# A post-norm decoder on one core: where the output bias is added to the residuals, and where two output pieces stand in the last attention unit

## Chip, cores, metric

One core of a Trainium2 chip. The metric is device time in microseconds of one execution, median of several runs; lower is better. TensorE (PE, with its weight loads PEld), VectorE (DVE), ScalarE (ACT), GpSimd (POOL) and SyncE (SP, which here issues nearly all DMAs) each run their own queue in order.

## The reference, cut to what matters

Four sequences (B=4) of 1024 tokens with 512 features, all float32:

```python
x = layernorm(x + attn(x))            # 32 channels of 16; q, k, v each two linear layers
x = layernorm(x + xattn(x, ctx, z0))  # causal convolution of two taps, LSTM-like gates
x = layernorm(x + ffn(x))             # x rounded to int8 steps, ternary weight, bias

def attn(x):
    q, k, v = (lin(lin(x, w, b), v_, c) for ...)          # split into 32 heads of 16
    o = softmax(q @ k.T / sqrt(16)) @ v
    return o.rearranged @ wo_w.T + wo_b                   # the output projection
```

The change touches `x + attn(x)`: the bias `wo_b` that is added to the residual `x`, and the pieces of the output projection; `layernorm` subtracts a mean and divides by a root.

## The kernel before

**Units.** Attention runs in 32 units u of four heads (L385): eight per batch. A unit has 32 half steps h (L822). In each, TensorE makes the natural scores of the *next* unit (`nat`, L555; VectorE takes their row maxima, L584, and from them L590 and L598 make the shifts that DMAs carry into the queries, L608 and L612) and the transposed scores of this unit (`scores`, L621; ScalarE takes the exponential, L649). Every fourth half step `weigh` (L654) multiplies a finished quarter with v (PE L664); its result is copied by ScalarE (L675) or added by VectorE (L677) into `o_sb`. Also every fourth half step, at h = 3, 7, ..., 31, one piece of other matmul work is taken from a list (L834 to L839): `v` projections, parts of the next q and k projections (`product`, L451), and, when these are used up from unit 24 on, pieces of the output projection (`out_piece`, L547).

**PSUM.** Transposed scores, weighings and all pieces take turns in four buffers of one pool (`ps_st`, L522), in the order of the program: whoever asks waits until the work that reads the buffer of four requests ago is done. The natural scores have two wider buffers (`ps_nat`), which the last unit uses for half of its scores (`stw`).

**Products.** `product` forms q and k projections by a Strassen scheme with seven products. ScalarE copies each out of PSUM (L477, L479), and GpSimd adds it to the others (L482 to L493). The products 2, 3 and 4 are copied into two `rooms` that take turns (L470 to L472), so a copy waits until GpSimd's sum from the room's former user is done. Unit 24 has seven such pieces and one output piece.

**Normalising.** A unit's `o_sb` is divided by its sums in four stages during the next unit (L840): sums out by DMA, reciprocals (L697), back by DMA in broadcast (L703), and at h=20 the product on GpSimd (L711) with the writing to HBM (L721).

**Residuals.** At h=5 of unit 24, `load_w_o`, `load_attention(0)` and `load_residual(0)` (L842 to L845) issue the transfers of the output weight, the attention output and x of batch 0; at h=5 of unit 28, the same for batch 2 (L858). `load_residual` (L93) issues the DMA of 2 MB and, for batches 0 and 2, records right behind it eight GpSimd additions of `b_o`, one for each tile of 128 tokens (L98 to L100). For batches 1 and 3 VectorE adds it later (L246). `project` (L233) runs the matmuls of an output piece and has VectorE add the result to the residual `y` (L247) and, at a tile's last piece, take statistics (L249). The first two tiles of batch 0 have two pieces of 256 columns, all others three of 176, 176 and 160 columns.

**Last unit.** Unit 31 has no next unit and runs 16 steps i with twice the scores each (L800). Its list `firsts` is the first norm of batch 0: the root on ScalarE at i=2 (`deviations`, L110, L117), which needs another function table than the exponential, and from i=3 on the normalising on VectorE (L118, L140, L121) and its sums and differences for the convolution (L185 to L191). At even i it weighs a quarter and does one output piece:

```python
if i % 2 == 0 and weighing:
    weigh(*weighing.pop(0))
...
if i % 2 == 0 and len(out_pieces) > 1:
    out_pieces.pop(0)()
if i > 1 and firsts:
    firsts.pop(0)()
```

GpSimd sums the convolution's weights (L170) in the first part of this unit. After it comes the tail: convolution, gates, second norm, feed-forward, third norm.

The order of the work within each engine's queue is that of these calls; nothing reorders it (`manual_schedule`, L326).

Of the kernel before, what the change touches and what calls it, by code (L numbers as in the profile page):

```python
# [19 lines left out]
NT = S // P  # L20
# [41 lines left out]
class Handed:  # L62
# [30 lines left out]
    def load_residual(self, b):  # L93
        nc = self.nc
        self.y[b] = self.tokens(b, f"y{b}")
        nc.sync.dma_start(self.y[b], self.a["x"][b].rearrange("(t p) f -> p t f", p=P))
        self.stats[b] = self.shared.tile([P, NT, 6], F32, tag=f"stats1_{b // 2}", name=f"stats1_{b}")
        if b % 2 == 0:  # L98
            for t in range(NT):
                nc.gpsimd.tensor_add(self.y[b][:, t, :], self.y[b][:, t, :], self.b_o)  # L100

    def means(self, stats, pool, name, t0=0, n=NT):
        mv = pool.tile(
# [148 lines left out]
def attention(ctx, tc, a, attn_d, ident, shared, hand):  # L252
    nc = tc.nc
# [23 lines left out]
    for i in range(2):  # L277
        t = (once if i else shared).tile([P, NT, NH * VW + 15], F32, tag=f"v_sb{i}", name=f"v_sb{i}")
# [9 lines left out]
    for n, pool in ((3, shared), (1, once)):  # L288
        t = pool.tile([P, 8 if n == 3 else 2, S], F32, tag=f"qk{n}", name=f"qk{n}")
# [13 lines left out]
    for n in range(2):  # L303
        t = shared.tile([P, 4, D + 1], F32, tag="u", bufs=2, name=f"x_sums{n}")
# [5 lines left out]
    for i in range(2):  # L310
        t = once.tile([P, 32], F32, tag=f"neg{i}", name=f"neg{i}")
# [4 lines left out]
    for i in range(2):  # L316
        t = rbcp.tile([P, S], F32, tag=f"rbc{i}", name=f"rbc{i}")
# [95 lines left out]
    def qk_pieces(p, which):  # L413

        parts = [(0, 176), (176, 176), (352, 176), (528, 176), (704, 160), (864, 160)]
        return [
            lambda pool=None, part=part: project(p, which, *part, packs[p][:, which, :], pool) for part in parts
        ]
# [78 lines left out]
    def products(p, which):  # L497


        rows = [(2 * p - 3, 2), (2 * p - 2, 2), (2 * p - 1, 2), (2 * p, 2)]  # L500
        if which == 1:
            rows = [(2 * p - 2, 22), (2 * p - 2, 26), (2 * p - 1, 4), (2 * p, 4)]
        for n, when in enumerate(rows):
            due.setdefault(when, []).append(lambda n=n: to_quadrants(2 * p + n, which, packs[which][:, n // 2, :]))
        return [
            [
                lambda part=part: product(p, which, *part)
                for part in parts
            ]
            for parts in (  # L510
                [(1, 0, 256), (1, 256, 256), (6, 0, 256), (6, 256, 256), (2, 0, 256), (2, 256, 256)],
                [(7, 0, 512), (5, 0, 512), (3, 0, 256), (3, 256, 256), (4, 0, 256), (4, 256, 256)],
            )
        ]
# [32 lines left out]
    def out_piece(b, t, c0, c1):  # L547
        pt = ps_st.tile([P, QW], F32, tag="st", name=f"po{b}_{t}_{c0}")
        hand.project(b, t, slice(c0, c1), pt[:, 0 : c1 - c0], quarters=True)
# [133 lines left out]
    def normalise(u, stage):  # L683
# [51 lines left out]
    out_pieces = [  # L735
        lambda b=b, t=t, c=c: out_piece(b, t, *c)
        for n, (b, t) in enumerate(outs)
        for c in ([(0, 256), (256, 512)] if n < 2 else [(0, 176), (176, 352), (352, 512)])
    ]
# [14 lines left out]
    for u in range(-1, NU):  # L754
        fill = []

        p, w = 2 * ((u + 5) // 4), (u + 1) % 4
        if p < NU // 2:
            if w % 2 == 0:
                parts = products(p, w // 2)  # L760
                if p == 14 and w == 0:


                    parts[0].pop()
                    parts[0].append(lambda: product(14, 0, 2, 256, 128))
                    parts[1].insert(0, lambda: product(14, 0, 2, 384, 128))
            fill += parts[w % 2]
        if u == -1:
            fill = folds[5:] + qk_pieces(1, 0) + qk_pieces(1, 1) + [
                piece for t in range(NT) for piece in v_pieces(0, t)  # L770
            ] + fill
        elif units[u][0] + 1 < B:
            vs = v_pieces(units[u][0] + 1, units[u][1])
            fill = fill + vs if w == 3 else vs + fill
        if w == 2 and p + 2 < NU // 2:
            due.setdefault((u, 24), []).append(lambda p=p: sum_w(p + 2, 0))
        if w == 0 and u >= 0 and p < NU // 2:
            due.setdefault((u, 24), []).append(lambda p=p: sum_w(p, 1))
        if w == 3 and p % 4 == 2 and p // 4 + 1 < B:
            due.setdefault((u, 28), []).append(lambda p=p: sum_x(p // 4 + 1))  # L780
        if u == -1:
            xts[1] = load_x(1)
        elif units[u][1] == 5 and units[u][0] + 2 < B:
            xts[units[u][0] + 2] = load_x(units[u][0] + 2)

        if u == -1:
            total, done, steps = len(fill), 0, HS // 3 + 1
            for n in range(steps):
                hs = range(3 * n, min(3 * n + 3, HS))
                for work in [nat(0, h // 2, h % 2, apart=h % 2 == 1) for h in hs]:  # L790
                    work()
                if n in (6, 7):
                    shift(0, 0, n == 6)
                until = total * (n + 1) // steps
                for piece in fill[done:until]:
                    piece()
                done = until
        elif u + 1 == NU:
            assert not fill
            for i in range(HS // 2):  # L800
                for work in [scores(u, i, i % 2), scores(u, i, 1 - i % 2, wide=True)]:
                    work()
                if i % 2 == 0 and weighing:
                    weigh(*weighing.pop(0))
                if i % 2 == 1:
                    weighing.append((u, i // 2))
                if i % 2 == 0 and len(out_pieces) > 1:
                    out_pieces.pop(0)()
                if i > 1 and firsts:
                    firsts.pop(0)()  # L810
                if i == 1:
                    hand.first_w = hand.load_conv(0, None)
                if i in (3, 5):
                    hand.load_ctx(i // 2 - 1)
                if i in (8, 9, 10, 11):
                    hand.sum_taps(hand.first_w, i - 8)
                if i < 2:
                    shift(u, 1, i == 0)
                if i in (2, 5, 8, 11) and stages:
                    stages.pop(0)()  # L820
        else:
            for h in range(HS):  # L822
                i, half = divmod(h, 2)
                for work in (nat(u + 1, i, half), scores(u, i, 1 - half)):
                    work()
                if h % 4 == 1 and weighing:
                    weigh(*weighing.pop(0))
                if h in (1, 3):
                    shift(u, 1, h == 1)
                if h in (17, 19):  # L830
                    shift(u + 1, 0, h == 17)
                for work in due.pop((u, h), ()):
                    work()
                if h % 4 == 3:  # L834
                    weighing.append((u, h // 4))
                    if fill:
                        fill.pop(0)()
                    elif u > 24 or u == 24 and h > 24:
                        out_pieces.pop(0)()  # L839
                if h in (5, 9, 13, 20) and stages:  # L840
                    stages.pop(0)()
                if h == 5 and u == 24:  # L842
                    hand.load_w_o()
                    hand.load_attention(0, big_slot(0, "big0"))
                    hand.load_residual(0)  # L845
                    hand.load_rest()
                if h == 5 and u == 27:
                    hand.load_w_f()
                if h == 21 and 27 <= u < 31:
                    hand.prepare_w_f(u - 27)  # L850
                if h == 21 and u == 29:
                    hand.prepare_rest()
                if h == 5 and u == 30:
                    hand.x1[0], firsts = hand.first_norm(0)
                    firsts.pop(0)()
                    hand.xf[0], parts = hand.fir_parts(0, hand.x1[0], shared)
                    firsts.extend(parts)
                if h == 5 and u == 28:  # L858
                    hand.load_attention(2, big_slot(1, "big2"))
                    hand.load_residual(2)  # L860
            assert not fill
        if u == -1:
            setup.close()
            atp = ctx.enter_context(tc.tile_pool(name="at", bufs=14))
            obuf = ctx.enter_context(tc.tile_pool(name="obuf", bufs=2))
            onp = ctx.enter_context(tc.tile_pool(name="onp", bufs=1))
# [332 lines left out]
```

## Time and profile before

| | |
|---|---|
| median of 3 runs | 2428.03 us (2427.8 to 2428.67) |
| the profiled execution | 2427.53 us, its span 2425.7 us, granted clock 0.999 |
| GpSimd: wait for the residual of batch 2 (L100 on DMA y) | 54.4 us, once |
| DMA of batch 0's residual: issued, first add | 1503.3 us, 1520.81 us |
| units 20, 24, 25, 28 (first exponential to first exponential) | 57.4, 63.4, 55.7, 57.3 us |
| ScalarE at L649, idle time before it for scores | 529.8 us in 497 waits |
| HBM traffic | 80.77 MB read, 18.35 MB written |

Rows of a time-ordered view have the start and the time taken, in us from the span's start, then engine, line of the kernel, operation, what is written and read, shapes, count, and in brackets the idle time of the engine just before and what ended it. Rows of the waits have us in total, times, and the longest. `part` is the PSUM tile of a product, `st` and `stw` are transposed scores, `nat` natural scores, `av` a weighing, `at` an exponential, `po` an output piece, `y` a residual, `extra` and `qk` the packed projections. A row "PE st L638 <- ACT extra L479" reads: TensorE's scores of L638 waited for ScalarE's copy of L479.

### The profile page before, as it was taken

To read this page: it belongs to the slowest core of one execution; us is meant where nothing else is said; L and a number is where in the kernel's file an instruction comes from. 1 tells how busy PE (TensorE), PEld (TensorE's weight loads), DVE (VectorE), ACT (ScalarE), POOL (GpSimd) and SP (SyncE) were. 2 spreads that over 40 slices of the span, in tenths; PEclk is the share of its full clock that TensorE was granted. 3 is DMA by queue.
4 is the path that set the end of the run, shared out by engine and by line. 5 is a ranking of instruction groups with operands and counts; after the bars stand their busy time and mean duration, and the time that the engine had idled before them with its cause. 6 is when DMAs were issued, how large, how long until landed. Compare 5 with 4: busy or idle time off the path is not lost.

```text
span 2425.7 us, 70210 instructions
## 1 busy us (share of the span) xinstructions
PE 2410.5 (99%) x30380; PEld 1626.6 (67%) x30380; DVE 1747.9 (72%) x2197; ACT 1329.0 (55%) x2593; POOL 588.5 (24%) x537
## 2 busy tenths in 40 slices
PE   9999999999999999999999999999999999999998
PEld 5556666666666666666666666566666799747994
DVE  3577777777777777777777777677777477878677
ACT  1056666666666666666666666566666723411333
POOL 5011311111122212111311201311210267422661
PEclk9999999999999999999999999999999999999999
DMA  6200112011001111111110012102200242160311
GB/s 222 59 3 17 28 23 56 17 30 26 17 17 30 21 54 22 25 21 20 27 25 17 17 34 93 41 17 48 89 17 12 81 149 87 70 226 18 122 35 70
DMA packets 80838, 121.45 MB, mean 50 GB/s; under 512 B 39072, under 2 KB 39328, under 8 KB 80528
## 3 DMA queue, kind: packets, MB, share of 16 engines
q1 hardware_dynamic: 79808, 115.77, 16.8%
q8 instruction: 239, 3.92, 0.7%
q10 hardware_dynamic: 720, 1.18, 0.1%
q14 instruction: 71, 0.58, 0.1%
HBM read 80.77 MB, written 18.35 MB: 41 GB/s over the span
## 4 chain that ended last, share of the span: by engine, by line
PE 97%; DVE 1%; POOL 0%; ACT 0%; DMA 0%; issue 0%; SPq 0%; DVEq 0%; POOLq 0%; ACTq 0%
PE nat L568 22%; PE av L664 20%; PE st L638 18%; PE part L59 8%; PE pc L948 6%; PE pa L948 6%; PE v L59 5%; PE pf L1032 4%; PE po L59 2%; PE po L241 2%; PE proj L59 1%; PE fold L377 1%; PE fold L59 1%; PE tr L1024 0%; PE nats L568 0%; POOL y L100 0%
## 5 line engine op out<-in xcount | busy, mean ns | idle before, releaser
L584 DVE TENSOR_REDUCE mx<-nat 128x2 f32<-128x1024 f32 x1008 | 1188.0, 1220 | 402.8 <-PE st L638 375.0
L649 ACT ACTIVATE at<-st 128x512 f32<-128x512 f32 x2016 | 1043.2, 603 | 541.6 <-PE st L638 529.8
L568 PE MATMUL nat<-qk 32*128 32x512 f32 x4032 | 1011.8, 614 | 0.5 <-DVE mx L584 0.5
L638 PE MATMUL st<-qk 32*128 32x256 f32 x8064 | 1002.0, 387 | 3.7 <-ACT extra L479 3.7
L638 PEld LDWEIGHTS st<-qk 32*128 32x128 f32 x8064 | 685.7, 184 | 48.8 <-ACT extra L479 4.5
L664 PE MATMUL av<-at,v_sb 128*32 128x256 f32 x8192 | 499.6, 383 | 1.4 <-ACT at L649 1.4
L568 PEld LDWEIGHTS nat<-qk 32*128 32x128 f32 x4032 | 344.0, 184 | 220.1 <-DVE mx L584 136.6
L664 PEld LDWEIGHTS av<-at,v_sb 128*32 128x32 f32 x8192 | 241.7, 110 | 223.1 <-ACT at L649 90.2
L948 PE MATMUL pc<-xf,w 128*128 128x171 f32 x1024 | 159.9, 308 | 0.6 <-DVE o_sb L677 0.6
L948 PE MATMUL pa<-xf,w 128*128 128x171 f32 x1024 | 159.8, 308 | 0.0
L948 PEld LDWEIGHTS pc<-xf,w 128*128 128x128 f32 x1024 | 152.0, 189 | 1.7 <-DVE o_sb L677 1.1
L948 PEld LDWEIGHTS pa<-xf,w 128*128 128x128 f32 x1024 | 152.1, 189 | 0.0
L711 POOL TENSOR_TENSOR o_n<-o_sb,rbc 128x512 f32<-128x512 f32 x64 | 97.7, 1547 | 170.9 <-DMA rbc<-rec_d 132.8
L959 ACT ACTIVATE u<-u,b_c 128x512 f32<-128x512 f32 x64 | 46.2, 721 | 161.1 <-DVE u L958 161.1
L59 PE MATMUL v<-w_v,xT 128*32 128x256 f32 x2048 | 121.7, 382 | 0.0
L1032 PE MATMUL pf<-w_f,xq_t 128*128 128x512 f32 (+1 forms) x264 | 115.2, 581 | 1.7 <-ACT xq_t L1026 1.5
L677 DVE TENSOR_TENSOR o_sb<-av,o_sb 128x256 f32<-128x256 f32 x128 | 54.4, 425 | 73.6 <-PE av L664 73.1
L170 POOL TENSOR_TENSOR w<-w 128x512 f32<-128x512 f32 x64 | 81.8, 1311 | 92.9 <-DMA w<-in_conv_wT 61.1
L482 POOL TENSOR_TENSOR qk<-qk 128x256 f32<-128x256 f32 x14 | 10.1, 724 | 380.1 <-ACT qk L479 379.9
L59 PEld LDWEIGHTS v<-w_v,xT 128*32 128x32 f32 x2048 | 61.1, 109 | 55.0 <-ACT at L649 16.5
L675 ACT COPY o_sb<-av 128x256 f32<-128x256 f32 x128 | 48.0, 375 | 78.0 <-PE av L664 63.4
L59 PE MATMUL part<-x_sums,w_sums 128*32 128x256 f32 (+1 forms) x896 | 83.6, 490 | 0.0
(139 smaller groups left out, 1810.4 us busy)
## 6 DMA issues: line engine op xcount, KB each, us to landing
w<-in_conv_wT SPq DMA_DIRECT2D x32, 512.0 KB
u<-in_ctx SPq DMA_DIRECT2D x16, 1024.0 KB
xT<-in_xT SPq DMA_DIRECT2D x16, 512.0 KB
qk<-qk SPq DMA_DIRECT2D x128, 64.0 KB
qk<-extra SPq DMA_DIRECT2D x128, 64.0 KB
rbc<-rec_d SPq DMA_DIRECT2D x128, 64.0 KB
attn<-o_n SPq DMA_DIRECT2D x256, 32.0 KB
big<-attn SPq DMA_DIRECT2D x4, 2048.0 KB
```

The lines of the kernel that those rows point to most:

```text
L59: nc.tensor.matmul(pt[r, :], lhsT(f)[:, r], rhs(f), start=f == 0, stop=f == tiles - 1)
L170: self.nc.gpsimd.tensor_tensor(w[:, i, tap, :], w[:, i, 0, :], w[:, i, 1, :], op)
L241: nc.tensor.matmul(pt, attn_t[:, f, t * P : (t + 1) * P], self.w_o[:, f, cols], start=f == 0, stop=f == FT - 1)
L568: nc.tensor.matmul(pts[n], q_ts[u % 4][r : r + 32, qt * P : (qt + 1) * P], k_ts[u % 4][r : r + 32, kh * 512 : kh * 512 + 512], start=True, ...
L584: nc.vector.tensor_reduce(mxs[u][:, qt, 2 * pair : 2 * pair + 2, kh], pt, AX.X, ALU.max, negate=True)
L638: nc.tensor.matmul(st[:, k * QW : k * QW + QW], k_ts[u % 4][r : r + 32, kt * P : (kt + 1) * P], q_ts[u % 4][r : r + 32, qq * QW : qq * QW ...
L649: nc.scalar.activation(at, st, AF.Exp, scale=0.25)
L664: nc.tensor.matmul(av[32 * j : 32 * j + 32, :], v_sb[b % 2][:, kt, c * VW : c * VW + 32], ats[u, 2 * i + n // 2, j][:, n % 2 * QW : n % 2 ...
L677: nc.vector.tensor_add(o, av, o)
L711: nc.gpsimd.tensor_mul(o_n[:, :, half * 256 : half * 256 + 256], o_sb[:, cols].rearrange("p (s e) -> p e s", e=2), rbc[:, cols].rearrange( ...
L948: nc.tensor.matmul(pt, w[:, i, tap, o : o + P], xf[:, tap, i, :], start=i == 0, stop=i == FT - 1)
L1032: nc.tensor.matmul(pt, xq_ts[b, t][:, f, :], hand.w_f[:, f, cols], start=f == 0, stop=f == FT - 1)
```

## The change

The eight additions leave `load_residual` and become a method that adds the bias to given tiles. The main loop calls it at half steps 25, 26, 29 and 30 of units 24 and 28, two tiles at a time, after the loop's other work of that half step. In the last unit the number of output pieces is 1 at even i as before, except 2 at i=2 and 0 at i=6. `self.nc` and the line numbers apart, nothing else differs: in the new order TensorE runs the same matmuls, with one piece of 160 columns moved from i=4 to i=2 and the following one, of 176 columns, from i=6 to i=4; GpSimd's sixteen additions stand later in its queue (in unit 24 four of them between the last two product sums, four behind; in unit 28 all eight behind L711 and the preparation of the feed-forward weight, L217); SyncE's queue is unchanged.

```diff
         self.stats[b] = self.shared.tile([P, NT, 6], F32, tag=f"stats1_{b // 2}", name=f"stats1_{b}")
-        if b % 2 == 0:
-            for t in range(NT):
-                nc.gpsimd.tensor_add(self.y[b][:, t, :], self.y[b][:, t, :], self.b_o)
+
+    def add_b_o(self, b, tiles):
+        for t in tiles:
+            self.nc.gpsimd.tensor_add(self.y[b][:, t, :], self.y[b][:, t, :], self.b_o)
...
                 if i % 2 == 1:
                     weighing.append((u, i // 2))
-                if i % 2 == 0 and len(out_pieces) > 1:
+
+                for n in range({2: 2, 6: 0}.get(i, 1 - i % 2)):
                     out_pieces.pop(0)()
...
                     hand.load_w_f()
+                if u in (24, 28) and h in (25, 26, 29, 30):
+                    n = (25, 26, 29, 30).index(h)
+                    hand.add_b_o((u - 24) // 2, (2 * n, 2 * n + 1))
```

## Prediction

> **What bounds the kernel now.** I read the page's busy line first, then who waits for whom on TensorE alone, then TensorE's, ScalarE's, VectorE's and GpSimd's rows in time order around each long wait. Page and waits of TensorE:
>
> ```profile
> PE 2410.5 (99%) x30380; PEld 1626.6 (67%) x30380; DVE 1747.9 (72%) x2197; ACT 1329.0 (55%) x2593; POOL 588.5 (24%) x537
> ...
> PE st L638 <- ACT extra L479: 3.7, 1, 3.7
> ...
> PE av L664 <- ACT at L649: 1.4, 1, 1.4
> ```
>
> TensorE is busy 2410.5 of 2425.7 us, so time can only come from its 15 us of gaps or from stretches in which its records are long. Two gaps stand out, each a single wait. The first, followed back along the chain that ended last (start, us, what):
>
> ```profile
> 1522.05 7.91 POOL y L100 x7
> ...
> 1530.00 1.23 POOL qk L486
> ...
> 1533.85 0.73 POOL qk L491
> ...
> 1534.61 0.38 ACT extra L479
> ...
> 1535.03 1.13 PE st L638 x6
> ```
>
> GpSimd stands at the head of its queue with the bias adds of L100 until the residual has landed (issued at 1503.3, first add at 1520.81), runs eight adds, and only then the sums of the Strassen products. The sum at 1533.85 frees one of the two rooms that ScalarE's copy of a product (L479) needs; behind that copy in ScalarE's queue are the exponentials, whose PSUM buffers the next scores need. TensorE's rows show the whole loss:
>
> ```profile
> 1521.58 1.07 PE L59 MATMUL part<-xT,w_sums 128*32 128x256 f32 x16
> ...
> 1528.32 1.07 PE L59 MATMUL part<-x_sums,w_qk 128*32 128x256 f32 x16
> ...
> 1535.03 1.13 PE L638 MATMUL st<-qk 32*128 32x256 f32 x6 [3.71 <-ACT extra L479]
> 1536.09 3.59 PE L664 MATMUL av<-at,v_sb 128*32 128x256 f32 x32
> ...
> 1541.54 1.07 PE L59 MATMUL part<-x_sums,w_qk 128*32 128x256 f32 x16
> ```
>
> ```profile
> core 0: us, PE busy (x) PEld busy (x) DVE busy (x) ACT busy (x) POOL busy (x), PEclk, DMA share, GB/s
> ...
> 1535.00:1540.00 5.00, 4.97 (x44) 2.50 (x48) 0.20 (x1) 1.95 (x4) 3.87 (x4) 0.66 0.07 16
> ```
>
> A product every four half steps: 1528.32 - 1521.58 = 6.74 us is the regular distance, and 1541.54 - 1528.32 = 13.22 us the one with the stall. It costs 6.48 us, not 3.71: the rest is the drained pipeline around it and the value matmuls behind it, 3.59 us where the same 32 take 1.93 elsewhere, because the granted clock (the 0.66 of the last row, for 1535 to 1540 us) fell to half for 3.4 us after the gap.
>
> The second long wait is in the last unit (u=31), and a smaller loss is in unit 28:
>
> ```profile
> 1899.49 1.28 ACT L117 ACT_TABLE_LOAD   x1
> ...
> 1902.40 1.09 ACT L649 ACTIVATE at<-st 128x512 f32<-128x512 f32 x2
> ...
> 1903.05 2.32 PE L664 MATMUL av<-at,v_sb 128*32 128x256 f32 x29 [1.42 <-ACT at L649]
> ```
>
> ```profile
> 1746.34 9.90 POOL L100 TENSOR_TENSOR y<-y,b_o 128x512 f32<-128x512 f32 x8 [54.38 <-DMA y<-in_x]
> ...
> 1748.02 0.88 DVE L590 TENSOR_TENSOR neg<-mx 128x16 f32<-128x16 f32 x1
> ...
> 1805.32 0.19 DVE L590 TENSOR_TENSOR neg<-mx 128x16 f32<-128x16 f32 x1
> ```
>
> ScalarE leaves the exponentials from 1899.49 to 1902.40 for the root and its two table loads; the weighing at 1903.05 waits for a buffer that the exponential at 1902.40 frees. In unit 28 the adds begin at 1746.34 and the small minimum of L590 takes 0.88 instead of 0.19 us.
>
> **Part 1: the adds of the first residual, unit 24.** Removed from the head of GpSimd's queue: one wait (to 1520.81) and eight adds (9.15 us). No transfer moves: the queue that issues DMAs has the same order before and after, so the residual still lands at 1520.8 and the row shifts and reciprocals behind it are where they were. In the new order of GpSimd's queue the product sums come first, each waiting only for its ScalarE copy, as in unit 20, where they follow the copy by hundredths of a microsecond and TensorE shows no gap. So the room is free when the copy of the product of 1528.32 comes, and the 6.48 us go. I take 6.5. The bounds: at least 3.7 (the gap alone, if the slow clock came anyway), at most 6.5.
>
> What is late next? In clock of the profile less the stall: the copy ends near 1530.0, its sum near 1530.8; four adds of 1.26 us end at 1535.9; the last product's copy ends near 1536.7 (it was 1543.2), its sum at 1537.5; four more adds end near 1542.5. Waiting behind these adds: that last sum, read by a transfer at half step 2 of unit 25, about 1544 and so 7 us later; the sums of unit 25, from about 1565 on; and VectorE, which adds the first output piece to the residual at 1550.34 - 6.5 = 1543.9 while tile 0 is ready at 1532. Ahead of the adds stands the normalising product L711, which waits for the reciprocals; it ran at 1535.21 with no idle time before it, so they had landed by then. Even with that latest landing tile 0 is ready at 1535.2 + 3.0 + 0.7 + 1.3 = 1540.2. Cost of all this: nothing, and with the cover gone one for one on VectorE from 1543.9.
>
> [...] Before, four of the adds ran while VectorE was heading for its own stall; now all lie beside its work. [...]
>
> **Part 2: the adds of the third batch's residual, unit 28.** No gap of TensorE hung on the wait for the transfer. But the collision at 1748 held up VectorE's L247 behind it and through it a scores buffer: from weighing to weighing (1742.56 to 1750.47) it took 7.91 us, and at the same place of units 27, 29 and 30, by the exponentials' starts, 7.27, 7.32 and 7.20. That is 0.65 us. In the new order L711 and the weight preparation come first; the reciprocals were issued from 1746.38 to 1748.1 and land about 2.2 us later (in unit 29 the issue ended at 1799.66 and L711 began at 1801.91), so L711 runs from about 1750.3, the preparation to 1754.8, the adds to about 1764.8. GpSimd is then idle at 1748.0, and no L590 falls in 1754.8 to 1764.8 (the next is at 1777). Readers come at unit 29, past 1790. Gain 0.65; bounds 0 (if it hits something I don't see) and 0.7.
>
> **Part 3: two output pieces at i=2, none at i=6.** One piece (32 matmuls, 160 columns, 1.29 us) goes in front of the root; its place at i=6 is empty. Scores to scores with the root is 1906.60 - 1899.49 = 7.11 us; with the same kind of piece and no root 1922.90 - 1917.54 = 5.36. So the root costs 1.75. With the piece ahead, scores of i=3 start near 1900.8 instead of 1899.49, the weighing of i=4 is ready at 1902.8 and still starts at 1903.05, since the exponential ends when it did: TensorE reaches i=5 at 1906.7, with a piece more done, where without change it is at 1906.60 with a piece less. Then i=5 and i=6 take about 3.95 us without a piece, so i=7 starts at 1910.65. ScalarE's work there is eight exponentials of about 0.48 us net and the copy L675, 4.3 us, from 1907.87 to 1912.16; that copy frees the buffer that the second scores of i=8 need, natural at 1911.45: a wait of 0.7. The weighing of i=8 starts near 1913.4 instead of 1914.14. Gain 0.7: 1.4 of the root's 1.75 covered, 0.7 given back. Bounds: 0 if ScalarE gives all of it back, 1.3 if the copy doesn't hold the scores. VectorE's extra L249 of 0.69 before the norm delays only work that is needed from 1938 on. [...]
>
> **Sum.** 6.5 + 0.65 + 0.7 = 7.85 us. Of the profiled execution (2427.53, span 2425.7) that leaves 2419.7; its own time is 0.5 under the median of 2428.03, from which I forecast 2420.2, 0.32% faster. A measurement tells about 0.2%, 4.9 us, from no change: 2423.2.
>
> **Rivals.**
> - Only the gap goes, the small parts give nothing (the slow clock comes anyway, or ScalarE and the port eat it): 2428.0 - 3.7 = 2424.3, and 2421.5 if the whole stall goes but nothing else. For the first: the clock's fall is a record of its own. Against: it is the only one in the body of the run and begins right after the gap. 5% for the first; the second is inside my case.
> - It doesn't do what it says: the product sums wait for something else in that stretch, so the stall stays: 2428.0 - 0.65 - 0.7 = 2426.7. Against: the chain above goes through the adds without a break, and unit 20 has the same sums without a stall. 4%.
> - Slower: the moved adds hold VectorE's reductions. Were all sixteen adds to block it for 1.26 us, that is 20 us, less the 28% of its time that is idle over the 20 us and the 7.85 gained: about 2428 + 20 - 6 - 8 = 2434. It decides from 12.7 us of blocking. Against: the reductions' 2.36 us under the adds of before. 2%.
> - My case, 2419 to 2422: 89%.
>
> Range 2418.8 to 2423.2: below, part 3 in full and 0.7 of unrecorded gain; above, the whole-stall-only case and its 0.7 of collision, and half of the way to the clock rival. Chances: faster by over 0.2% 0.90 (my case and a little of the first rival), within 0.2% 0.08, slower 0.02.
>
> **What would show it.** In the changed profile: no wait of TensorE for L479 near 1531 and products 6.74 us apart throughout unit 24, clock 1.00 there; L486 within a microsecond of its ScalarE copy; L590 at 0.19 in unit 28; in the last unit a weighing that starts at 1903.05 - 7.15 with under 0.3 of wait, and about 0.7 of wait of the scores of i=8 for L675. I am wrong if a wait of similar length appears for VectorE's L247 on GpSimd, if the clock still falls in unit 24, or if L590 at its half step 31 is long.

## The result and the profile after

The changed kernel takes 2418.95 us (median of 7 runs, 2418.2 to 2420.07). The kernel before takes 2426.23 us (7 runs, 2424.51 to 2428.67: the three of the table above and four more). The ratio is 0.9968, that is 0.32% faster; its 95% interval, here and below in square brackets, is [0.9958, 0.9978]. The profiled execution took 2419.16 us, its span 2417.4 us, where that of before had 2425.7. Line numbers are one higher than before up to L805, and five higher in the tail.

The page's busy line, and below it the waits of TensorE (total us, times, longest us):

```profile
PE 2406.9 (100%) x30380; PEld 1625.5 (67%) x30380; DVE 1745.3 (72%) x2197; ACT 1328.8 (55%) x2593; POOL 586.8 (24%) x537
```
```profile
PE pf L1037 <- ACT xq_t L1031: 1.5, 2, 0.8
...
PE av L665 <- ACT at L650: 0.3, 1, 0.3
```

The row of 3.7 us on ScalarE's copies of the products is gone, and the wait of the last unit's weighing went from 1.4 to 0.3. In unit 24, TensorE's rows in time order:

```profile
1521.35 1.07 PE L59 MATMUL part<-xT,w_sums 128*32 128x256 f32 x16
...
1528.08 1.07 PE L59 MATMUL part<-x_sums,w_qk 128*32 128x256 f32 x16
...
1531.02 1.93 PE L665 MATMUL av<-at,v_sb 128*32 128x256 f32 x32
...
1534.81 1.07 PE L59 MATMUL part<-x_sums,w_qk 128*32 128x256 f32 x16
```

The products stand 6.73 us apart, twice (13.22 before at the stall), and the weighing between them has the regular 1.93 us instead of 3.59. The stretch of 5 us that had clock 0.66 has 1.00 (columns: time, total us, then busy us and count of PE, PEld, DVE, ACT, POOL, then clock, DMA share, GB/s):

```profile
1535.00:1540.00 5.00, 5.00 (x78) 3.07 (x74) 3.77 (x4) 3.77 (x9) 3.55 (x5) 1.00 0.02 3
```

GpSimd's queue shows why. Its sums now run when their copies come, and each waits for nothing else; the adds (L101) stand in the free time between them:

```profile
1502.11 1.27 POOL L487 TENSOR_TENSOR qk<-qk 128x512 f32<-128x512 f32 x1 [7.36 <-ACT qk L478]
...
1524.69 2.99 POOL L712 TENSOR_TENSOR o_n<-o_sb,rbc 128x512 f32<-128x512 f32 x2 [0.90 <-DMA rows_d<-turned]
1529.80 0.72 POOL L494 TENSOR_TENSOR qk<-qk,extra 128x256 f32<-128x256 f32 x1 [2.13 <-ACT extra L480]
1530.49 4.60 POOL L101 TENSOR_TENSOR y<-y,b_o 128x512 f32<-128x512 f32 x4
1536.54 0.72 POOL L494 TENSOR_TENSOR qk<-qk,extra 128x256 f32<-128x256 f32 x1 [1.45 <-ACT extra L480]
1537.22 4.59 POOL L101 TENSOR_TENSOR y<-y,b_o 128x512 f32<-128x512 f32 x4
...
1743.66 2.97 POOL L712 TENSOR_TENSOR o_n<-o_sb,rbc 128x512 f32<-128x512 f32 x2 [57.20 <-DMA rows_d<-turned]
...
1748.05 9.90 POOL L101 TENSOR_TENSOR y<-y,b_o 128x512 f32<-128x512 f32 x8
...
1797.87 1.49 POOL L218 TENSOR_SCALAR w_f<-w_f 128x512 f32<-128x512 int32 x1
```

The first sum ran at 1502.11; before, it stood behind the adds until 1529.96. VectorE's small minimum has its short time in unit 28. In unit 29 it takes 0.49 us, 0.17 us after the start of the weight preparation of 1797.87; before, it came there 0.45 us after that start (1805.32 against 1804.87) and took 0.19:

```profile
1741.42 0.19 DVE L591 TENSOR_TENSOR neg<-mx 128x16 f32<-128x16 f32 x1
...
1798.04 0.49 DVE L591 TENSOR_TENSOR neg<-mx 128x16 f32<-128x16 f32 x1
```

Last unit, TensorE: the weighing behind the root, which waited 1.42 us before.

```profile
1895.97 2.32 PE L665 MATMUL av<-at,v_sb 128*32 128x256 f32 x29 [0.34 <-ACT at L650]
```

Where the difference between the two spans comes from, by the distances of the same work in the two traces: unit 24 (first exponential to first exponential) 63.37 to 56.88, **-6.49**; the step of unit 28 with the minimum (weighing to weighing) 7.91 to 7.22, **-0.70**; units 27, 29 and 30 together **+0.35**; the last unit (first scores to the tail's first matmul) 48.89 to 47.81, **-1.08**. What remains, -0.24 ahead of unit 24 and -0.2 in the tail, lies where the change does nothing. Together that is -8.4 us; the spans, each rounded to a tenth, differ by 8.3.

### The profile page after: what moved, and what is told of

Same layout as the page of the kernel before. It is cut to its first block, busy times and chain, and to the rows that moved or that the text cites. A ratio compares the mean times of both kernels' runs of the same rounds, so it can differ in the third digit from the quotient of the medians.

```text
span 2417.4 us, 70215 instructions
## 1 busy us (share of the span) xinstructions
PE 2406.9 (100%) x30380; PEld 1625.5 (67%) x30380; DVE 1745.3 (72%) x2197; ACT 1328.8 (55%) x2593; POOL 586.8 (24%) x537
## 4 chain that ended last, share of the span: by engine, by line
PE 99%; DVE 0%; ACT 0%; issue 0%; DVEq 0%; ACTq 0%
PE nat L569 22%; PE av L665 20%; PE st L639 19%; PE part L59 8%; PE pc L953 6%; PE pa L953 6%; PE v L59 5%; PE pf L1037 4%; PE po L59 2%; PE po L242 2%; PE proj L59 1%; PE fold L378 1%; PE tr L1029 1%; PE fold L59 1%; PE nats L569 0%; PE idle_ps L341 0%
```

## The experiments

**The theory**: the adds at the head of GpSimd's queue end too late for the sums behind them; the rooms stay full; TensorE stalls and its clock falls. Take the adds from the head, or let the residual land early enough, and the stall goes whole. **The rivals**: the clock falls whether or not there is a gap (then only 3.7 us go); the moved adds hold VectorE, so that leaving them out gains more; in part 3, ScalarE gives back what the piece covers. The stall of a profile is the length of its unit 24 less 56.88 us, which is the length in every profile without a gap of TensorE there.

### Before, once more

No edit.

> The kernel before, profiled once more. It asks whether the stall of unit 24 has a fixed size: the runs of before spread over 4 us, those of the changed kernel over less than 2. If the stall depends on when the residual's transfer lands, the distance of the products in unit 24 is 10 to 13.5 us here and follows the start of the first bias add; if it is fixed by the adds alone, it is 13.2 +- 0.1 whatever the start. Ratio 1.000 +- 0.001.

Measured: 2427.39 us (12 runs, 2424.9 to 2429.63), ratio 1.0001 [0.9993, 1.0009]. The products stand 14.17 us apart (1527.66 and 1541.83), which is in neither of the two answers: the stall has another size than the one the forecast was built on. TensorE's rows, then the clock by stretches of 5 us:

```profile
1533.71 1.72 PE L638 MATMUL st<-qk 32*128 32x256 f32 x6 [3.05 <-ACT extra L479]
1535.37 3.64 PE L664 MATMUL av<-at,v_sb 128*32 128x256 f32 x32
```
```profile
1530.00:1535.00 5.00, 1.95 (x11) 0.88 (x6) 2.19 (x2) 1.67 (x4) 4.92 (x5) 0.91 0.00 0
1535.00:1540.00 5.00, 5.00 (x44) 2.28 (x46) 0.42 (x1) 0.89 (x2) 2.55 (x3) 0.50 0.14 34
1540.00:1545.00 5.00, 5.00 (x66) 3.37 (x62) 3.35 (x3) 3.25 (x7) 0.73 (x1) 0.91 0.09 23
```

The gap does follow the first add: that add comes 32.12 us after the unit's first exponential instead of 32.79, and the gap is 0.66 us shorter. Yet the stall is 7.44 us instead of 6.49: the clock lacks 0.09, 0.50 and 0.09 of three stretches, which at half speed is (0.09 + 0.50 + 0.09) x 5 x 2 = 6.8 us of slow clock, where the first profile had 3.4. And the minimum of unit 28 took 0.19 us though it ran under the adds: they are eight from 1747.07 to 1757.0, so the second begins near 1748.3, and the minimum of 1748.30 fell on that border. In unit 29, on the other hand, where the first profile had 0.19, it now takes 0.37, under a weight preparation that began at 1804.63:

```profile
1748.30 0.19 DVE L590 TENSOR_TENSOR neg<-mx 128x16 f32<-128x16 f32 x1
...
1804.91 0.37 DVE L590 TENSOR_TENSOR neg<-mx 128x16 f32<-128x16 f32 x1
```

So the unchanged kernel has no fixed loss in unit 24, 28 or 29.

### Each part alone

Part 1 alone; its mirror image is part 2 alone:

```diff
-                if u in (24, 28) and h in (25, 26, 29, 30):
+                if u == 24 and h in (25, 26, 29, 30):
...
                     hand.load_residual(2)
+                    hand.add_b_o(2, range(NT))
```

> Only the adds of unit 24 are moved; unit 28 and the last unit are as before. Theory: the half-step stall goes in full, products 6.74 us apart, clock 1.00 in unit 24; -6.5 us in a profile (5 to 6.5 if the stall varies), ratio 0.9973 to 0.9979. Rival, the clock falls anyway: -3.7 us, 0.9985.

Measured: 2420.57 us (8 runs, 2419.79 to 2421.64), ratio 0.9971 [0.9961, 0.9982]. By the medians that is 7.06 us, a little more than the 5 to 6.5 that were expected. Unit 24 takes 56.88 us, the clock stays at 1.00, and the last unit's wait is back in full (1.4 us).

> Only the adds of unit 28 are moved. Theory: nothing of TensorE hung on that wait; the small minimum in unit 28 is back at 0.19 us and the step at 7.2 instead of 7.91, but units 29 and 30 can lose a few tenths where the normalising product meets the same minimum: -0.7 to 0 us, ratio 0.9997 to 1.0000. Rival, the 54 us wait of GpSimd held something up: -2 us or more.

Measured: 2426.67 us (13 runs, 2424.04 to 2429.64), ratio 0.9996 [0.9988, 1.0005], not told from no change. The minimum's step is 7.22 us as forecast, but this profile has the largest stall of all, 8.61 us behind a gap of 4.22, again with 6.8 us of slow clock:

```profile
1534.38 1.95 PE L639 MATMUL st<-qk 32*128 32x256 f32 x6 [4.22 <-ACT extra L480]
```

Part 3 alone is the kernel before with one line:

```diff
-                if i % 2 == 0 and len(out_pieces) > 1:
+                for n in range({2: 2, 6: 0}.get(i, 1 - i % 2)):
                     out_pieces.pop(0)()
```

> Only the output pieces of the last unit are moved. The prediction's sum gives -0.7 us (ScalarE gives 0.7 of 1.4 back at i=8), the profile after -1.05. Last unit from its first scores to the first convolution matmul 48.9 before: 48.2 by the prediction, 47.8 by the profile after. Ratio 0.9996 to 0.9998.

Measured: 2425.86 us (13 runs, 2422.64 to 2427.78), ratio 0.9993 [0.9985, 1.0001]. By the times that is not told from nothing, because the stall is still there and varies by more. By the trace the last unit takes 47.80 us, as in the changed kernel, where 48.2 had been the prediction's figure, and TensorE's wait is the changed kernel's 0.3. The minimum, still under the adds of unit 28, took more than in any other profile:

```profile
1747.48 1.31 DVE L590 TENSOR_TENSOR neg<-mx 128x16 f32<-128x16 f32 x1
```

### The landing or the place in the queue

The adds stay at the head of the queue, but the residual is asked for ahead of the output weight and the attention output; the rest is the kernel before.

```diff
                 if h == 5 and u == 24:
+                    hand.load_b_o()
+                    hand.load_residual(0)
                     hand.load_w_o()
                     hand.load_attention(0, big_slot(0, "big0"))
-                    hand.load_residual(0)
```

> The kernel before with the adds left at the head of GpSimd's queue in unit 24; only the order of the transfers is changed: bias and residual of batch 0 are issued ahead of the output weight and the attention output. Theory (the stall is the wait for the landing plus the adds, less the slack of the sums): the residual lands near 1510 instead of 1520.8, the adds end near 1520, the product sums catch up before the room is needed at 1529, and the stall goes: -6.5 us, 0.9973. Rival (the eight adds in front of the sums make the stall, not the landing): no change, 1.000.

Measured: 2420.16 us (8 runs, 2419.62 to 2420.68), ratio 0.9975 [0.9965, 0.9985]. GpSimd runs the eight adds at the head, 8.7 us earlier in the unit than in the first profile (24.05 us after its first exponential instead of 32.79), and catches up before the rooms are needed:

```profile
1511.26 9.15 POOL L102 TENSOR_TENSOR y<-y,b_o 128x512 f32<-128x512 f32 x8 [17.12 <-DMA y<-in_x]
...
1529.23 0.73 POOL L495 TENSOR_TENSOR qk<-qk,extra 128x256 f32<-128x256 f32 x1 [0.53 <-ACT extra L481]
```

Unit 24 takes 56.89 us. The place in the queue is not harmful in itself; what counts is when the last add ends. In the first profile the adds ended at 1529.92 and the sum that frees the room ended 4.6 us later, while ScalarE was free for the copy that wants the room from 1529.7 on (it then waited 4.91 us for that sum): the adds had to end by about 1525, in the time of that profile.

The next edit fixes the point: six adds at the head, two behind (the rest as before).

```diff
                     hand.load_residual(0)
+                    hand.add_b_o(0, range(6))
...
+                if u == 24 and h == 25:
+                    hand.add_b_o(0, (6, 7))
```

> The kernel before with six of the eight adds of unit 24 left at the head of GpSimd's queue, two moved behind the product sums; all else as before. Four profiles with eight at the head fit stall = gap + 1.0 + half of the slow clock's stretch (3.4 or 6.8 us). Two adds less (2.3 us) leave a gap of 0.8 to 1.9. If a gap of that length does not bring the clock down, the stall is 1.8 to 2.9 us and unit 24 is 58.7 to 59.8 us long, ratio 0.9978 to 0.9985; if the clock falls all the same, it is 60.4 to 63.2 us.

Measured: 2422.88 us (13 runs; 12 of them 2421.04 to 2424.47, one 2427.35), ratio 0.9989 [0.9981, 0.9997]. The six adds end at 1520.35 + 6.88 = 1527.2; this trace is 0.18 us ahead of the first profile at that place, so they are 2.4 us past the deadline. The stall is 2.32 us: a gap of 1.19, and a weighing behind it at full speed. Unit 24, 59.20 us long, is as forecast; the ratio is a little above the forecast's 0.9985 (in this profile the minimum of unit 28, still under its adds, took 1.17 us).

```profile
1532.34 1.12 PE L639 MATMUL st<-qk 32*128 32x256 f32 x6 [1.19 <-ACT extra L480]
1533.39 1.93 PE L665 MATMUL av<-at,v_sb 128*32 128x256 f32 x32
```
```profile
1535.00:1540.00 5.00, 5.00 (x72) 3.42 (x64) 3.42 (x4) 2.89 (x7) 4.19 (x5) 1.00 0.21 53
```

The clock follows the gap: it stays at 1.00 here. The run at 2427.35 has no profile, but its mean granted clock was 0.998, where the others had 0.999 to 1.0; a longer gap with a slow stretch would fit, and is not shown.

### What do the moved adds cost?

The bias of batches 0 and 2 left out altogether; the rest is the changed kernel.

```diff
-                if u in (24, 28) and h in (25, 26, 29, 30):
-                    n = (25, 26, 29, 30).index(h)
-                    hand.add_b_o((u - 24) // 2, (2 * n, 2 * n + 1))
```

> The changed kernel without the sixteen bias adds: the bias is left out of batches 0 and 2. It prices the moved adds. If they are free where they stand now, it is equal to the changed kernel within 0.3 us (ratio to before 0.9966 to 0.9969); if they hold VectorE or delay sums, it is faster by more than 1 us.

Measured: 2418.18 us (6 runs, 2417.82 to 2418.82), ratio 0.9967 [0.9955, 0.998]; unit 24 takes 56.88 us, as with the adds. Sixteen adds beside VectorE's work cost nothing there, and in the times nothing that can be told.

The adds put two half steps later in unit 24, so that they run under its last small minimum (the calls for unit 28 stay):

```diff
+                if u == 24 and h in (27, 28, 29, 30):
+                    hand.add_b_o(0, (2 * h - 54, 2 * h - 53))
```

> The changed kernel, but all eight adds of unit 24 stand behind the last product sum, so that they run from 1537.3 to about 1546 and lie over VectorE's small minimum at 1543.4. If VectorE is blocked for the rest of a running add, the minimum takes 0.3 to 1.3 us instead of 0.19 and the step of half steps 29 to 32 grows by up to 0.7; TensorE loses 0.3 to 0.7 us against the changed kernel, ratio to before 0.9969 to 0.9972. If the moved adds cost nothing wherever they lie: as the changed kernel.

Measured: 2418.63 us (6 runs, 2418.43 to 2419.29), ratio 0.9968 [0.9957, 0.998]. GpSimd's and VectorE's rows:

```profile
1535.83 9.17 POOL L101 TENSOR_TENSOR y<-y,b_o 128x512 f32<-128x512 f32 x8
```
```profile
1541.78 0.98 DVE L591 TENSOR_TENSOR neg<-mx 128x16 f32<-128x16 f32 x1
```

The minimum is held (0.98 instead of 0.19), and unit 25 then takes 56.14 instead of 55.65 us: 0.49 us, too little for the times to show.

To take away the collision that the changed kernel's profile shows in unit 29, the feed-forward weight is prepared between the adds of unit 28:

```diff
                     hand.add_b_o((u - 24) // 2, (2 * n, 2 * n + 1))
-                if h == 21 and 27 <= u < 31:
-                    hand.prepare_w_f(u - 27)
+                    if u == 28:
+                        hand.prepare_w_f(n)
```

> The changed kernel with the four preparations of the feed-forward weight taken from behind the normalising products of units 27 to 30 and put between the adds of unit 28. Theory: they or the product in front of them meet VectorE's small minimum; with them gone from there the minimum of unit 29 is at 0.19 us and its step at 7.3 instead of 7.61; unit 27 keeps what its product costs: -0.2 to -0.4 us against the changed kernel. If the minimum is held by the product alone, no change.

Measured: 2418.23 us (6 runs, 2417.28 to 2418.66), ratio 0.9969 [0.9957, 0.9981]. VectorE:

```profile
1797.70 0.19 DVE L591 TENSOR_TENSOR neg<-mx 128x16 f32<-128x16 f32 x1
```

In units 27 to 30 no minimum takes more than 0.19 us, and unit 29 takes 56.59 instead of 56.90. That the edit did it is not shown. In unit 29 the normalising product ended at 1797.14, so a preparation right behind it would have begun 0.56 us before the minimum, and in four other profiles a minimum that came 0.45 to 0.59 us into a preparation took 0.19 as well; in unit 27 the minimum came at the end of the product by chance. The medians of the times differ from the changed kernel's by 0.7 us, which the intervals do not separate.

### The empty slot of the last unit

The slot without a piece at i=14 instead of i=6, to see whether ScalarE's copy at i=8 gives anything back.

```diff
-                for n in range({2: 2, 6: 0}.get(i, 1 - i % 2)):
+                for n in range({2: 2, 14: 0}.get(i, 1 - i % 2)):
```

> The changed kernel with the missing output piece at i=14 instead of i=6. If the empty place at i=6 cost something because ScalarE has not yet caught up there, this gives 0.2 to 0.4 us more; if any empty place costs the same, it is equal within 0.1; if the end of the unit is the worse place (the last weighings wait for ScalarE), it loses up to 0.7.

Measured: 2418.39 us (5 runs, 2417.57 to 2418.75), ratio 0.9967 [0.9954, 0.9979]; the last unit takes 47.80 us, the changed kernel's 47.81. Where the empty slot lies makes no difference.

### The changed kernel, once more

No edit to it.

> The changed kernel once more. Unit 24 at 56.88 us, last unit at 47.8, unit 28's step at 7.2; runs within 2 us of each other, where those of before spread over 4 or more because the gap and the slow clock's stretch vary. Ratio 0.9968 +- 0.0008.

Measured: 2418.88 us (7 runs, 2417.45 to 2419.32), ratio 0.9971 [0.9961, 0.9982]. Unit 24 takes 56.88 us and the step of unit 28 7.22, as expected; unit 27 takes 56.56 us and unit 29 56.67, where the first profile of the same kernel had 56.78 and 56.90. All 14 runs of the changed kernel lie within 2.6 us; all 89 runs of the kernel before lie within 7.5 us (2422.77 to 2430.28, median 2427.0). The change takes the spread away with the stall: part 1 alone (8 runs) and the early residual (8 runs) stay within 1.9 us.

## Why the prediction was right or wrong, point by point

**The whole.** The forecast ratio was 2420.2 / 2428.03 = 0.9968, and so it was measured; that the last digit agrees is partly luck. The time, 2418.95 us, is 1.25 us lower than forecast and at the low edge of the range. Most of that is the level it was taken from: three runs had the median 2428.03, seven have 2426.23, all 89 have 2427.0. And in the first pair of profiles two misses cancel: part 3 brought 0.38 us more than forecast, units 27, 29 and 30 together cost 0.35 that the sum did not have. The mechanism was right in all three parts; the steps that failed are two terms of the sum, the stall of part 1 and what part 3 gives back.

**Part 1: mechanism right, size taken for fixed.** Each sign came: no wait for the copy, 6.73 us between products, clock 1.00, sums on the heels of their copies. The early residual and six adds at the head show that the end of the adds decides. What failed is the sentence "at most 6.5": it took the stall of one profile for the stall. In the four profiles with all eight adds at the head and the landing as before it is 6.1 to 8.6 us. These four, and the one with six adds (us; "first add" counts from the unit's first exponential):

| | first add | gap | slow clock | gap + 1.0 + half the slow clock | stall measured |
|---|---|---|---|---|---|
| the first profile of before | 32.79 | 3.71 | 3.4 | 6.4 | 6.49 |
| before, once more | 32.12 | 3.05 | 6.8 | 7.45 | 7.44 |
| part 2 alone | 33.28 | 4.22 | 6.8 | 8.6 | 8.61 |
| part 3 alone | 32.41 | 3.34 | 3.4 | 6.05 | 6.10 |
| six adds at the head | 32.51 | 1.19 | 0 | 2.2 | 2.32 |

The 1.0 is fitted to the rows with eight adds; that it is the drained pipeline around the gap is a reading, not shown. So the stall varies for two reasons. The gap follows the start of the first add, and so, as the early residual shows, the landing of the transfer, one for one: first add less gap is 29.06 to 29.08 us in all four profiles with eight adds. And the slow clock behind it lasts 3.4 or 6.8 us; where it lasts 6.8, the gain is 7.4 to 8.6. Why the landing varies by 1.2 us is not known.

**The clock rival** fell: no kernel without the gap has a slow stretch there, and a gap of 1.19 us brought none.

**Part 2: the mechanism was right, the 0.65 a draw.** In six profiles of kernels that leave the adds of unit 28 at the head, the minimum took 0.88, 0.19, 1.31, 0.28, 1.17 and 1.17 us, and its step 7.91, 7.22, 8.34, 7.31, 8.20 and 8.21; so what is to be gained is 0 to 1.1 us, by where in an add it falls. The price of the part was thus a single draw as well, which happens to lie at the mean of the six (0.65). The 0.30 us that unit 29 lost between the two profiles, and the 0.14 of unit 27, are draws of the same kind and not shown to be a price of the change: in unit 29 the minimum took 0.37, 0.49 and 0.34 us in three of the five other profiles with unit 28's adds at the head, and 0.41 in the kernel without any adds. The row of 0.19 at 1805.32, which the prediction took for the undisturbed case, was itself 0.45 us into a weight preparation.

**Part 3: two terms mis-sized, in sum too pessimistic.** Forecast 0.7, measured 1.08. The weighing started as forecast (1903.05 - 7.15 = 1895.90; it was 1895.97, with 0.34 of wait). The scores of i=5 and i=7, which stood at 1906.60 and 1912.07 before:

```profile
1899.63 0.48 PE L639 MATMUL st<-qk 32*128 32x256 f32 x2
...
1903.91 0.48 PE L639 MATMUL st<-qk 32*128 32x256 f32 x2
```

From i=5 to i=7 TensorE needs 4.28 us instead of 5.47: the empty slot saves 1.19, where the prediction's 3.95 us meant 1.52. From i=7 to i=9 it needs 5.46 us (1903.91 to 1909.37), before 5.47. So the step that failed is "0.7 given back" at i=8: nothing is given back there, and TensorE's waits have none for the copy L675. 1.19, less 0.10 for the wider piece at i=4, is the gain to 0.01 us. With the slot at i=14 it is there that a step is 1.19 shorter. The prediction took pieces by the time of their rows (1.29 for 160 columns), but a piece's matmuls overlap their neighbours: by the distance of the steps, 160 columns are worth 1.08 us (which is also what the added piece takes off the wait at i=4, 1.42 to 0.34), and 16 columns more 0.11.

In the changed kernel two table loads of 1.28 us and the root of 0.30 kept ScalarE from the exponentials from 1892.42 to 1895.33, 2.91 us, as long as before (1899.49 to 1902.40).

**The slower rival** fell: the kernel without the adds has the same unit 24 (56.88 us). Under GpSimd's adds the small minimum took up to 1.31 us instead of 0.19; the reductions (2.36 us for two at 1523.76 in the first profile of before; in the changed kernel 2.35 at 1530.26 under the adds and 2.36 at 1520.59 without them) and L677 (0.42 at 1533.09 in the changed kernel) kept their times. No run shows the 0.7 us of collision that the upper end of the range adds to the whole-stall case: in the changed kernel the minimum of unit 24 took 0.19, at 1543.18, 1.37 us behind the last moved add, and laid under the adds it took 0.98, with 0.49 us lost in unit 25. That a port holds the minimum, as the first rival has it, is not shown; the runs show only how long it took.

**Open**: the run at 2427.35 with six adds at the head; why the landing of the residual and the length of the slow clock vary; and the 0.4 us of the two spans' difference that lie outside the changed places.

## What to carry to other kernels

An instruction that waits for a DMA at the head of an in-order queue costs nothing until its end passes the moment when the work behind it is due (here eight adds that ended at 1520.41 left unit 24 at 56.89 us, and six that ended 2.4 us too late cost 2.32); work that moment out (here about 1525), then either move the instruction behind or bring the transfer forward, and both are worth the same (here ratios of 0.9971 and 0.9975). A stall read from one profile is one draw of it: take a second profile of the kernel before, and see whether its loss varies, before calling it a bound. And take the worth of a piece of work from the distance of the steps with and without it: its rows overlap with the work beside it (160 columns here: 1.29 us by the rows, 1.08 by the steps).

## What the runs showed of the hardware

Gaps of TensorE of 3.05, 3.34, 3.71 and 4.22 us were each followed by half the clock (0.50), for 6.8, 3.4, 3.4 and 6.8 us, so the length doesn't follow that of the gap; a gap of 1.19 us was followed by none.

A VectorE minimum of two small inputs in SBUF, 0.19 us by itself, took up to 1.31 us under GpSimd's adds of 1.1 to 1.3 us: in the first profile of before it ended at 1748.89, 0.04 us after the add that it had met. In that profile the second add of the row begins 1.25 us after the first; by that distance, two minima started within 0.02 us of the start of a second add, and one took 0.19 (1748.30, before once more, row from 1747.07), the other 1.31 (1747.48, part 3 alone, row from 1746.24). Under the weight preparation of 1.49 us (int32 to float32) it was held only to 0.65 us after that had begun, not to its end. In unit 29 of seven profiles it came 0.06, 0.16, 0.17, 0.18, 0.24, 0.28 and 0.31 us after the start and took 0.59, 0.49, 0.49, 0.48, 0.41, 0.37 and 0.34 us: it ended 0.65 or 0.66 us after the start each time. In four others, where it came 0.45 to 0.59 us after the start, it took 0.19. What holds it, and why for another length than under the adds, is not shown.
